# Graph-network layer in fp32: edge blocks turned in 32 by 32 squares on VectorE, and the last 24 blocks dealt singly by a clock of estimates

## The chip, the cores and the metric

The kernel runs on one core of a Trainium2 chip. The metric is the device time of one execution in microseconds (us). Before the change the median of three runs is 1333.0 us (1331.73 to 1334.65).

The core has several engines that run side by side and meet at semaphores: TensorE (PE in the profile; its weight loads are PEld), VectorE (DVE), ScalarE (ACT), GpSimd (POOL) and SyncE (SP, which here only issues transfers). Each engine takes its instructions in the order in which they were written into its own program. An instruction that waits holds up all that stand behind it on that engine.

## The reference

There are 8192 nodes with 256 channels, and 131072 edges sorted by their target node, each with 64 attributes. Cut to what matters:

```python
ea = edge_attr @ w_e + b_e
msg = relu(x[src] + ea)                       # gather of source rows
agg = segment_sum(msg, dst, num_segments=N)   # sum by target
t = x + agg
h_local = bn1(relu(t @ w1 + b1) @ w2 + b2 + x)
h_attn  = bn2(attention(x, groups of 32 nodes, 4 heads) + x)
out = h_local + h_attn
out = bn3(out + relu(out @ m_w1 + m_b1) @ m_w2 + m_b2)
return layernorm(x + out)
```

All of it is computed in float32.

## The kernel before

**Edges.** The 131072 edges are cut into 128 blocks of 1024 (`NB`, `BE`). A block's edges lie on 128 partitions in 4 groups `h` with 2 columns `j` each. For each block the kernel does this:

- `gather` (L134): 8 indirect transfers issued by GpSimd, each fetching 128 source rows of 1 KB into the tile `xs`. There are 4 such tiles in rotation, so the gather of block b+4 can't begin before block b has been added up. From block 20 (`NX`) on the rows come from `xb`, a copy of x with the edge bias already added, which the kernel makes in the first blocks (`copy_load`, `copy_store`, L547 to L553).
- `load_edges` (L149): the attributes of two blocks in one transfer of 512 KB from SP, in pieces of 512 bytes.
- `edge_transpose` (L167, L169): the matrix product needs attributes on partitions and edges along the row. TensorE turns the 4 groups of a block against the identity into a PSUM tile `tp`, and ScalarE copies them out to `eaT`.
- `edge_products` (L459; below block 20 also L467 for the bias): `eaT` times the edge weights, into two PSUM tiles `pe` of two banks each.
- `edge_messages` (L481, L485): VectorE adds `pe` and `xs` into `msg`, ScalarE applies the relu. Two additions a block; for the very last block four smaller ones.
- `edge_hot` (L490), `edge_sums` (L504, L510): TensorE multiplies a one-hot matrix of the targets with `msg`, which sums the edges of up to 32 neighbouring targets in each group (`pw`). ScalarE copies it to `ws`.
- `edge_place` (L522, L532): a second one-hot product moves the sums to their place among 160 node columns (`l2`), and VectorE adds them to `xT`, the transposed node features.

**Nodes.** The 8192 nodes are cut into 16 chunks of 512. For each chunk there are three generators: `attention_front` (L276 to L297), `attention_back` (L308 to L375) and `dense` (L391 to L444: the two local layers, the two layers of the MLP, the layer norm and the store). `dense` of a chunk can start once the last block that touches it has been placed. The last two chunks are cut into pieces: (14, tiles 0 to 2), (14, 2 to 4), (15, 0 to 2), (15, 2 to 3) and (15, 3 to 4).

**Order.** The program order of TensorE is the order in which this code calls (`manual_schedule`), that of VectorE and ScalarE is by hand only below block 26 (`NV`) and later left to a scheduler. The loop (L640 to L683) takes blocks in pairs, and the last 8 (`NS`) singly: products, additions, sums of the blocks before, products and additions of the second block, then node work, the turning of blocks b+2 and b+3, the placing, more node work. How much node work stands between is a budget in estimated microseconds (`Work.run`, 5.1 us a block, 4.2 below block 20), handed round the generators in turn.

**PSUM.** Eight banks: 2 for `at` (node work), 4 for `pe`, 1 shared by `tp` and `pw` (tag `sm`), 1 for `l2`.

Of the kernel before, what the change touches and what calls it, by code (L numbers as in the profile page):

```python
# [9 lines left out]
FP = mybir.dt.float32  # L10
# [8 lines left out]
P = 128  # L19
N, C, E, ED, H, NPG = 8192, 256, 131072, 64, 4, 32  # L20
DH = C // H
KC = C // P
BE = 1024
NB = E // BE
# [3 lines left out]
TB = NH * TJ  # L28
NPB = N // NB
# [10 lines left out]
NS = 8  # L40
# [11 lines left out]
def gnn_kernel(ctx: ExitStack, tc: tile.TileContext, x, src, dst, edge_attr, w, out):  # L52
# [7 lines left out]
    for b in range(ND):  # L60
        (nc.sync, nc.scalar)[b].dma_start(
            srcd[:, b * NH : (b + 1) * NH, :], src[b * BE : (b + 1) * BE].rearrange("(g p j) -> p g j", p=P, j=TJ)
        )
# [56 lines left out]
    def bank():  # L120
        return pps.tile([P, CH], FP, name="at", tag="at", bufs=2)
# [22 lines left out]
    def load_edges(b):  # L144

        if b % 2:
            return
        ea = epool.tile([P, 2, NH, TJ * ED], FP, name="ea", tag="ea", bufs=2)
        nc.sync.dma_start(  # L149
            ea.rearrange("p s h d -> p (s h) d"),  # L150
            edge_attr[b * BE : (b + 2) * BE, :].rearrange("(g p j) d -> p g (j d)", p=P, j=TJ),
        )
        for s in range(2):
            ea_of[b + s] = ea[:, s]
# [4 lines left out]
    load_edges(2)  # L159
# [3 lines left out]
    def edge_transpose(b):  # L163
        ea = ea_of.pop(b)
        tp = pps.tile([P, NH, P], FP, name="tp", tag="sm", bufs=1)
        for h in range(NH):
            nc.tensor.transpose(tp[:, h, :], ea[:, h, :], ident)  # L167
        eaT = epool.tile([P, NH, P], FP, name="eaT", tag="eaT", bufs=2)
        nc.scalar.copy(eaT, tp)  # L169
        eaT_of[b] = eaT  # L170

    with tc.tile_pool(name="setup", bufs=1) as sp:
# [17 lines left out]
        edge_transpose(0)  # L190
        edge_transpose(1)
        srcf = npool.tile([P, NH, P, TJ], FP, name="srcf", tag="zT")
        nc.vector.tensor_copy(srcf.rearrange("s h p j -> s (h p j)"), srci_r)
        for h in range(NH):
            ps = bank()[:, : TJ * NB].rearrange("p (j s) -> p j s", j=TJ)
            for j in range(TJ):
                nc.tensor.transpose(ps[:, j, :], srcf[:, h, :, j], ident)
# [33 lines left out]
        dstf = npool.tile([P, NH, P, TJ], FP, name="dstf", tag="oT")  # L231
        nc.vector.tensor_copy(dstf.rearrange("s h p j -> s (h p j)"), dsti_r)

        dst3 = dstf.rearrange("s h p j -> s h (p j)")
# [5 lines left out]
        for h in range(NH):  # L240
            ps = bank()[:, : TJ * NB].rearrange("p (j s) -> p j s", j=TJ)
            for j in range(TJ):
                nc.tensor.transpose(ps[:, j, :], dstf[:, h, :, j], ident)
# [205 lines left out]
    pe_of, msg_of, oh_of = {}, {}, {}  # L449

    def edge_products(b):

        eaT = eaT_of.pop(b)
# [361 lines left out]
```

## Time and profile before

| | |
|---|---|
| median of 3 runs | 1333.0 us |
| the profiled execution's own time | 1332.57 us |
| its span, first to last instruction | 1330.7 us |
| first gather starts, last gather's issue ends | 3.31 us, 1299.76 us |
| last row of the layer norm written (L441) | 1327.06 us |
| PE busy | 1234.3 us (93%) |
| DVE, ACT busy | 712.2 us (54%), 658.7 us (49%) |
| GpSimd busy in its 1024 gathers | 982.8 us of the three gather groups |
| mean TensorE clock granted | 0.986 of full speed |

Busy times add up over the whole span, and engines overlap. A busy share says little on what sets the end: an engine with a share of 74% can be the one that never stops, if the rest of its time is the gap between two of its own instructions that nothing else causes. The view of waits tells this: idle time put down to "issue" is time in which the engine waited for nothing that the profile shows.

### The profile page before, as it was taken

To read this page: it belongs to the slowest core of one execution; us is meant where nothing else is said; L and a number is where in the kernel's file an instruction comes from. 1 tells how busy PE (TensorE), PEld (TensorE's weight loads), DVE (VectorE), ACT (ScalarE), POOL (GpSimd) and SP (SyncE) were. 2 spreads that over 40 slices of the span, in tenths; PEclk is the share of its full clock that TensorE was granted. 3 is DMA by queue.
4 is the path that set the end of the run, shared out by engine and by line. 5 is a ranking of instruction groups with operands and counts; after the bars stand their busy time and mean duration, and the time that the engine had idled before them with its cause. 6 is when DMAs were issued, how large, how long until landed. Compare 5 with 4: busy or idle time off the path is not lost.

```text
span 1330.7 us, 21178 instructions
## 1 busy us (share of the span) xinstructions
PE 1234.3 (93%) x8307; PEld 783.6 (59%) x8307; DVE 712.2 (54%) x1202; ACT 658.7 (49%) x959; POOL 983.9 (74%) x1032
## 2 busy tenths in 40 slices
PE   4998979999999999899899999999898998989997
PEld 3766756655555556556556565555555565655665
DVE  4566554555537464644637464564636446454654
ACT  2535344465546455455546555463545445544443
POOL 7777777777777777777777777777777777777770
PEclk9998989999999999999999999999999999999999
DMA  8788655454545454454545454454445445444540
GB/s 279 251 277 272 198 149 151 135 159 130 168 137 153 135 166 126 132 170 125 165 137 150 138 169 136 121 169 138 151 138 151 135 138 150 136 136 139 159 116 30
DMA packets 140613, 206.77 MB, mean 155 GB/s; under 512 B 19646, under 2 KB 103900, under 8 KB 139740
## 3 DMA queue, kind: packets, MB, share of 16 engines
q0 software_dynamic: 49152, 134.28, 35.0%
q1 hardware_dynamic: 89468, 69.76, 16.8%
q10 hardware_dynamic: 1888, 1.32, 0.3%
q8 instruction: 67, 1.10, 0.3%
q14 instruction: 38, 0.31, 0.1%
HBM read 188.51 MB, written 16.78 MB: 154 GB/s over the span
## 4 chain that ended last, share of the span: by engine, by line
PE 56%; POOL 17%; issue 9%; DVE 8%; ACT 6%; DMA 4%; DVEq 0%; ACTq 0%; POOLq 0%
POOL xs L134 17%; PE at L391 16%; PE pe L459 11%; PE at L294 6%; PE pw L504 5%; PE l L522 3%; PE at L372 3%; DVE msg L481 3%; PE at L308 3%; PE tp L167 3%; PE pe L467 3%; DMA xs<-xb,srci 2%; PE at L360 2%; ACT pr L335 2%; DVE bd L352 1%
## 5 line engine op out<-in xcount | busy, mean ns | idle before, releaser
L134 POOL DMA_INDIRECT xs<-xb,srci x864 | 824.9, 955 | 263.8 <-issue 249.8
L485 ACT ACTIVATE msg<-msg 128x1024 f32<-128x1024 f32 (+1 forms) x258 | 270.9, 1051 | 329.5 <-DVE msg L481 320.7
L481 DVE TENSOR_TENSOR msg<-pe,xs 128x1024 f32<-128x1024 f32 (+1 forms) x258 | 304.7, 1211 | 174.5 <-PE pe L459 72.3
L459 PE MATMUL pe<-we,eaT 64*128 64x256 f32 x2048 | 262.3, 391 | 12.0 <-DVE msg L481 11.1
L459 PEld LDWEIGHTS pe<-we,eaT 64*128 64x128 f32 x2048 | 187.3, 187 | 99.7 <-issue 43.5
L134 POOL DMA_INDIRECT xs<-in_x_dram,srci x144 | 142.1, 987 | 45.3 <-issue 41.1
L391 PE MATMUL at<-hA,mw 128*128 128x512 f32 (+2 forms) x304 | 123.6, 533 | 3.4 <-ACT xT L284 2.0
L504 PE MATMUL pw<-msg,oh 128*32 128x256 f32 x2048 | 124.6, 382 | 0.0
L169 ACT COPY eaT<-tp 128x512 f32<-128x512 f32 x128 | 74.3, 581 | 100.0 <-PE tp L167 99.4
L294 PE MATMUL at<-xT,inT 128*128 128x512 f32 x256 | 122.7, 605 | 1.1 <-ACT xT L284 1.1
L391 PE MATMUL at<-m,mw 128*128 128x512 f32 (+2 forms) x304 | 117.4, 530 | 1.4 <-ACT m L407 1.4
L532 DVE TENSOR_TENSOR xT<-l,xT 128x352 f32<-128x352 f32 (+4 forms) x98 | 43.2, 463 | 96.0 <-PE l L522 96.0
L167 PEld LDWEIGHTS tp<-ident,ea 128*128 128x128 f32 x512 | 63.8, 144 | 49.9 <-issue 39.3
L504 PEld LDWEIGHTS pw<-msg,oh 128*32 128x32 f32 x2048 | 59.6, 109 | 54.6 <-issue 21.9
L167 PE MATMUL tp<-ident,ea 128*128 128x128 f32 x512 | 80.0, 280 | 11.8 <-DMA ea<-in_edge_attr_dram 6.1
L522 PEld LDWEIGHTS l<-oh,ws 128*128 128x128 f32 x512 | 74.1, 191 | 14.9 <-issue 13.5
L522 PE MATMUL l<-oh,ws 128*128 128x160 f32 x512 | 81.8, 301 | 0.5 <-ACT ws L510 0.5
L391 PEld LDWEIGHTS at<-m,mw 128*128 128x128 f32 x304 | 53.8, 190 | 48.0 <-issue 43.8
L391 PEld LDWEIGHTS at<-hA,mw 128*128 128x128 f32 x304 | 52.6, 190 | 49.1 <-issue 39.2
L294 PEld LDWEIGHTS at<-xT,inT 128*128 128x128 f32 x256 | 46.1, 192 | 50.2 <-issue 47.2
L391 PE MATMUL at<-xT,w 128*128 128x512 f32 (+2 forms) x152 | 64.8, 558 | 10.1 <-DVE y L431 4.7
L391 PE MATMUL at<-h,w 128*128 128x512 f32 (+2 forms) x152 | 65.5, 554 | 9.1 <-ACT h L398 6.4
(109 smaller groups left out, 1286.9 us busy)
## 6 DMA issues: line engine op xcount, KB each, us to landing
ea<-in_edge_attr_dram SPq DMA_DIRECT2D x64, 512.0 KB
xs<-xb,srci POOLq DMA_INDIRECT x864
xn<-in_x_dram SPq DMA_DIRECT2D x16, 512.0 KB
out_dram<-y SPq DMA_DIRECT2D x14, 512.0 KB
xp<-in_x_dram SPq DMA_DIRECT2D x10, 512.0 KB
xb<-xp SPq DMA_DIRECT2D x10, 512.0 KB
xp<-in_x_dram SPq DMA_DIRECT2D x3, 1024.0 KB
xb<-xp SPq DMA_DIRECT2D x3, 1024.0 KB
```

Of the source, the lines that this page charges most:

```text
L134: nc.gpsimd.indirect_dma_start(out=xs[:, h, j, :], out_offset=None, in_=x if b < NX else xb[:, :], in_offset=bass.IndirectOffsetOnAxis(ap= ...
L167: nc.tensor.transpose(tp[:, h, :], ea[:, h, :], ident)
L169: nc.scalar.copy(eaT, tp)
L294: nc.tensor.matmul(ps, inT[:, k, o * P : (o + 1) * P], xT[:, k, :], start=(k == 0), stop=(k == KC - 1))
L308: nc.tensor.matmul(ps[:, (t - t0) * C : (t - t0 + 1) * C], xT[:, k, t * P : (t + 1) * P], inT[:, k, 2 * C :], start=(k == 0), stop=(k == K ...
L391: nc.tensor.matmul(ps, wt[:, k, o * P : (o + 1) * P], act[:, k, :], start=(k == 0), stop=(k == nk - 1))
L459: nc.tensor.matmul(pe[:, i, u, :], eaT[rows, h + u, :], we[rows, :], start=(b >= NX or u == 0), stop=(b >= NX), skip_group_check=True,)
L481: nc.vector.tensor_add(msg[:, hs].rearrange("p u i c -> p i u c"), pe[:, :, u : u + n, :], xs[:, hs].rearrange("p u i c -> p i u c"),)
L485: nc.scalar.activation(msg[:, hs], msg[:, hs], AF.Relu)
L504: nc.tensor.matmul(pw[h * WN : (h + 1) * WN, i, :], oh[:, h * TJ + j, :], msg[:, h, j, :], start=(j == 0), stop=(j == TJ - 1), skip_group_ ...
L522: nc.tensor.matmul(l2[:, k, i * NPB : i * NPB + WB], ws[:, i, k * P : (k + 1) * P], oh2[:, i, :], start=(i == 0 and k == 0), stop=(i == la ...
L532: nc.vector.tensor_add(xT, l2[:, :, a - n : z - n], xT)
```

## The change

Four things change.

1. **Turning.** `edge_transpose` becomes one VectorE instruction per block, which turns each 32 by 32 square within its own 32 partitions; TensorE's 512 turnings, ScalarE's 128 copies and the PSUM tile `tp` go. That gives the wanted transpose only if the squares already stand on the right partitions: edge h*256 + j*128 + r*4 + m of a block stands in row r of two groups of 32 partitions, one for each half of the 64 attributes, and m and h count along the row. So `load_edges` now loads each block alone in 4 transfers of 32 partitions. Both halves are loaded by a transfer of the full rows, the second one shifted by 32 columns, so each attribute is fetched twice, in pieces of 1 KB. The index arrays (`srcd`, `srcf`, `dstf`) follow the new numbering; `srcd` is loaded in 8 transfers of single 4-byte elements where 2 transfers of 8-byte ones stood.
2. **PSUM.** The banks: 3 for `at` (2 before), 4 for `pe`, and 1 shared by `pw` and `l2`.
3. **The order up to block 103.** Turning of block b+2 now follows the products of block b at once (`next_edges`), and the placing stands at one place in each pair. The condition that a chunk's front waits for the placing of the chunk three before is dropped.
4. **The order from block 104 (`TAIL`) on.** Blocks go singly. A clock `t` of estimates is kept: `came` is when a block's rows are taken to have arrived, and each step of a block (products, additions, sums, placing) has an estimated due time. Whichever is due is written next; in between, `Work.step` writes one piece of node work. The additions of a block are put behind the newest copy of `ws` (ScalarE) and the newest addition to `xT` (VectorE) by `issue_after`.

```diff
-        return pps.tile([P, CH], FP, name="at", tag="at", bufs=2)
+        return pps.tile([P, CH], FP, name="at", tag="at", bufs=3)
...
+        ea = ea_of[b] = epool.tile([P, QR + NH * EQ * ED], FP, name="ea", tag="ea", bufs=2)
+        for j in range(TJ):
+            for i in range(ED // QR):
+                p0, c0 = j * ED + i * QR, (1 - i) * QR
+                nc.sync.dma_start(
+                    ea[p0 : p0 + QR, c0 : c0 + NH * EQ * ED].rearrange("r (g d) -> r g d", g=NH),
+                    edge_attr[b * BE : (b + 1) * BE, :].rearrange("(g j r m) d -> j r g (m d)", j=TJ, r=QR, m=EQ)[j],
+                )
...
-        tp = pps.tile([P, NH, P], FP, name="tp", tag="sm", bufs=1)
-        for h in range(NH):
-            nc.tensor.transpose(tp[:, h, :], ea[:, h, :], ident)
-        eaT = epool.tile([P, NH, P], FP, name="eaT", tag="eaT", bufs=2)
-        nc.scalar.copy(eaT, tp)
-        eaT_of[b] = eaT
+        eaT = eaT_of[b] = epool.tile([P, NH * EQ, QR], FP, name="eaT", tag="eaT", bufs=2)
+        nc.vector.transpose(eaT, ea[:, QR:].rearrange("p (g d) -> p g d", d=ED)[:, :, :QR])
...
+    def next_edges(b):
+        if b < NB:
+            edge_transpose(b)
+        if b + 2 < NB:
+            load_edges(b + 2)
...
-        l2 = pps.tile([P, KC, C], FP, name="l2", tag="l2", bufs=1)
+        l2 = pps.tile([P, KC, C], FP, name="l2", tag="pw", bufs=1)
...
+        came = [11.5 + 10.06 * (i + 1) for i in range(NB)]
+        t, p, m, s, l = came[b - 2] + 20, b, b, b - 2, b - 2
+        added = dict((i, came[i] + 2.0) for i in range(b))
...
+        while l < NB:
+            times = [1e9] * 4
+            if l < s:
+                times[0] = summed_at[l] + 1.5
+            elif s < m:
+                times[1] = max(added[s] + 1.2, bank_free)
+            if p < NB and m == p:
+                times[2] = added[p - 1]
+            if m < p:
+                times[3] = came[m]
+            if t >= times[0]:
+                edge_place(*sums)
...
+            elif t >= times[1]:
+                sums = edge_sums([s])
...
+            elif t >= times[2]:
...
+                edge_products(p)
+                next_edges(p + 2)
+                edge_hot(p)
...
+            elif t >= times[3]:
+                with ExitStack() as behind:
+                    for i in newest.values():
+                        behind.enter_context(tc.issue_after(i))
+                    edge_messages(m)
...
+            else:
+                t = work.step(t, min(times))
```

## The prediction

> **What bounds the kernel now.** I read the groups first. The row of the gathers carries the answer:
>
> ```profile
> L134 POOL DMA_INDIRECT xs<-xb,srci x864 | 824.9, 955 | 263.8 <-issue 249.8
> L459 PE MATMUL pe<-we,eaT 64*128 64x256 f32 x2048 | 262.3, 391 | 12.0 <-DVE msg L481 11.1
> L167 PE MATMUL tp<-ident,ea 128*128 128x128 f32 x512 | 80.0, 280 | 11.8 <-DMA ea<-in_edge_attr_dram 6.1
> L169 ACT COPY eaT<-tp 128x512 f32<-128x512 f32 x128 | 74.3, 581 | 100.0 <-PE tp L167 99.4
> ```
>
> Almost all the idle time before a gather is "issue". The view of GpSimd's waits says the same, and shows the one place where gathers waited for a free buffer:
>
> ```profile
> POOL xs L134 <- issue: 295.5, 970, 0.3
> POOL xs L134 <- DVE oh L513: 3.8, 6, 1.7
> POOL xs L134 <- DMA srcd<-in_src_dram: 1.7, 1, 1.7
> ```
>
> Then GpSimd's timeline, at the first gather, at block 18 and at the last:
>
> ```profile
> 3.31 1.10 POOL L134 DMA_INDIRECT xs<-in_x_dram,srcd  x1 [1.70 <-DMA srcd<-in_src_dram]
> ...
> 191.03 0.97 POOL L134 DMA_INDIRECT xs<-in_x_dram,srci  x1 [1.70 <-DVE oh L513]
> ...
> 1298.82 0.94 POOL L134 DMA_INDIRECT xs<-xb,srci  x1 [0.30 <-issue]
> ```
>
> From start to start a gather takes 1.25 us in the undisturbed stretches. 1024 of them from 3.31 us on would end at 1283; they end at 1299.76, so 16 us are lost to disturbances in all. This stream never stops, so before 1299.76 no other engine sets the time, PE with its 93% included: what PE saves there only makes the lag behind the gathers smaller. The end is the gather stream plus what follows it. Of the 30.9 us that follow (1330.7 - 1299.76), 3.64 are the last store and the close of the program (last row 1327.06, span 1330.7). The other 27.3 are work, and the timeline of the end shows how it stands:
>
> ```profile
> 1301.82 2.00 PE L459 MATMUL pe<-we,eaT 64*128 64x256 f32 x16
> 1303.75 1.07 PE L504 MATMUL pw<-msg,oh 128*32 128x256 f32 x16
> 1305.87 0.81 PE L522 MATMUL l<-oh,ws 128*128 128x160 f32 x4 [0.46 <-ACT ws L510]
> 1311.29 1.07 PE L504 MATMUL pw<-msg,oh 128*32 128x256 f32 x16
> 1314.46 0.71 PE L522 MATMUL l<-oh,ws 128*128 128x160 f32 x4
> 1315.20 0.39 DVE L532 TENSOR_TENSOR xT<-l,xT 128x224 f32<-128x224 f32 x1 [0.19 <-PE l L522]
> 1319.44 2.61 PE L391 MATMUL at<-hA,mw 128*128 128x128 f32 x16
> 1326.65 0.41 DVE L441 TENSOR_SCALAR y<-y,mv,rstd 128x256 f32<-128x256 f32 x1
> ```
>
> The rows of block 127 have landed at 1301.25 (last packet of the gathers' queue), but its products come only at 1301.82, its messages are complete at about 1306.3, its sums wait until 1311.29 behind node work written ahead of them, and it is placed at 1315.6. That is 14 us from landing to placed.
>
> **What the Trainium skill says.** "SBUF — State Buffer", section "Who interferes with whom", says that a VectorE instruction with one SBUF input outside the 2-port modes does not contend with GpSimd, while one with two SBUF inputs does contend with a GpSimd instruction that reads SBUF. The trace agrees: a fit of all 1024 gather spacings against what VectorE ran meanwhile gives 0.46 us lost per us of the additions at L552 (two SBUF inputs; 5.6 us in all) and 0.014 for the 64 square-turns at L352. "Perfetto Trace Analysis", section "GPSIMD Engine Instruction", says to time GpSimd by start-to-start spacing, as I did. "VectorE: DVE Perf Modes", section "The three transpose paths", says that VectorE turns 32 by 32 squares only, which is why the layout changes too; the time comes from L352, 701 ns at 512 elements a partition. "DMA: Bandwidth & Descriptors", section "Specifications", puts the least size for full rate at 512 bytes. The trace doesn't show a sharp edge there: packets of 512 bytes on SP's queue took 28.5 ns, of 1024 bytes 50.4.
>
> **The change part by part.**
>
> *Turning.* PE loses 512 x 0.28 = 80 us busy (4 of them take 0.66 us, so some 84), ScalarE 74 us, VectorE gains 128 x 0.70 = 90 us (712 becomes 802, 60% of the span). None of this is on the gather stream, which covers it. What reaches the stream: 90 us of new VectorE time at 0.014 is 1.3 us at most, zero at least; I take 0.7. In the first 60 blocks PE was the late engine: at block 18 the additions came 24 us after the rows, and the gathers of blocks 18 and 22 waited 1.70 and 0.85 us where 0.30 is usual. Those two waits, 1.95 us together, should go, since PE saves 0.66 us per block, 9 us by block 14. Against it, VectorE must turn block b+2 between the products and the additions of b, so the second additions come 0.7 us later; the sums (1.86 us) stand on PE meanwhile, so about 0.4 us a pair comes back. Bounds: 0 to -2.
>
> *Loads.* Each block takes 512 packets as before, twice as long: 512 x (50.4 - 28.5) ns / 16 engines = 0.7 us of 10 in DMA share, from 0.50 to 0.57 in the middle, from 0.85 to 0.92 in the first 60 us. SP issues 8 transfers a pair instead of 1, at about 0.4 us each; SP waits most of the time, so hidden. If not, edges come late, and the stream notices only when a lag of three blocks is used up.
>
> *Start.* This lies on the stream. The first gather waited for one `srcd` transfer, issued from 0.75 to 1.20 us. Now it waits for two on each of two queues, so for a second issue of about 0.45 us. The elements for block 0 are 1024, as many as both old transfers had together (9 ns each). I take +0.4, bounds +0.2 and +1.2. Behind these stand the loads that the third block's indices need (`srci_r`, landed about 12.6, `dsti_r` 15.5). Eight attribute transfers, each waiting for an earlier transfer (SP's waits show the custom: L178 stood 1.7 us for `we`), now stand ahead of them on SP, which puts them about 2 us later; a cast with a strided read and three casts follow. Before, the last was done at 20.5 and needed at 23.97. So 1.5 us of slack remain: 0 taken, up to +2 if it is used up.
>
> *Order to block 103 and PSUM.* No instruction is added. A third `at` bank and a single `pw`/`l2` bank move waits on PE, which the stream covers; 0.
>
> Gather end: 1299.76 + 0.4 - 1.95 + 0.7 = 1298.9. The 13 copy additions collide with gathers by chance, which may be 3 us either way.
>
> *The tail.* In the written order of the new program, TensorE's last items are: products 127, sums 126, 4 matmuls, placing 126, first layers of piece (15, 2 to 3), sums 127, 4 matmuls, placing 127, the rest. I time it on the old landing, 1301.25. Three of the four small additions of block 127 need only earlier rows, so after landing remain one addition (0.62), a relu (0.63) and about 0.3 of signals: 1302.8. But the mlp matmuls written before the sums need two operations that stand behind that addition on VectorE (0.35 each): sums at 1303.5 to 1304.5, `ws` copy (0.37) to 1305, placing behind 4 matmuls (1.16) from 1305.7 to 1306.4, addition to `xT` (0.39) done at 1306.9, against 1315.6. After that the old program needs 3.8 us to the mlp of the last piece (1315.65 to 1319.44) and 7.6 more to the last row. The new one writes more of piece (15, 2 to 3) in between: 0.6 first layer, 0.6 mlp, 0.6 first layer, 1.1 second mlp layer, 0.6 second layer, 1.1 mlp, 0.6 second layer, 0.4 turning, plus 0.5 of latency, 6.1 instead of 3.8. So 1306.9 + 6.1 + 7.6 = 1320.6: the last row 20.8 us after the last gather issue instead of 27.3, a gain of 6.5. What was late, the placing of block 127, is no longer; next late is PE itself with two pieces to finish. Bounds of the gain: 1 (the order stalls, below) and 9 (the last piece's matmuls run as tightly as before).
>
> *Sum.* 1298.9 + 20.8 + 3.64 = a span of 1323.3 us. The profiled execution took 1332.57 with a span of 1330.7, so 1.9 lie around it; the median of the runs, 1333.0, is 2.3 over the span. Predicted: 1325.6. What a measurement of this kernel can tell from no change is about 0.2%, 2.7 us: 1330.3 to 1335.7.
>
> **Rivals.**
>
> *The order doesn't fit the arrivals.* The clock takes block 127 to come at 1299.2, block 103 at 1057.7; the old trace has 1301.25 and 1060.2. If that holds, TensorE reaches products and sums two us early and stands, with ready node work behind it; VectorE stands too, at the second addition of each block. PE has 10 us a block and, by the written list, up to 9.8 us of work, so lost time piles up over some blocks. For it: PE can't overtake. Against: a constant offset is lost once, and pieces of node work fall due in between. Then about 1 to 5 us of the gain remain: 1327 to 1332, likeliest 1330.
>
> *A faster stream as well.* If the copy additions collide less and the start costs nothing, 1298.9 becomes 1295 to 1297, and with a tail gain of 7 the time is 1319 to 1323. For it: 5.6 us of collisions are there to lose. Against: their number does not change.
>
> *Slower: the new turns hold up GpSimd.* They are wider than those at L352 (128 partitions, 32 there) and read with a stride. If they cost the stream as the additions at L552 do, it is 90 x 0.46 = 41 us: 1366. It decides for "slower" from (7.4 + 2.7) / 90 = 0.11 us per us on. Against: 64 turns in the trace began and ended over gathers almost without a trace. Late edges in the first 20 blocks, with DMA near its full share, would end on the same side, but would need over 10 us of waits on the stream.
>
> **How the numbers follow.** Forecast (1323 to 1328.5): 0.60. Faster stream: 0.14. Misfit order: 0.16, half of it below 1330.3. Slower: 0.10. So faster 0.60 + 0.14 + 0.08 = 0.82, same 0.08, slower 0.10. The range takes the forecast, most of the faster stream and of the misfit: 1319.5 to 1332.
>
> **What would show it.** Right: gathers 1.25 us apart, no gap over 0.3 at blocks 18 and 22, last issue ending at 1297 to 1301; a start at about 3.7; 128 turns of about 0.7 us; block 127 placed 6 to 8 us after its last gather's issue ended (15.8 before); last row about 21 us after it. Wrong: gathers stretched while VectorE turns; a wait for `srci` near 24 us; waits of TensorE for additions of VectorE in each block after 104; idle PE in the last 20 us.

## The result, and the profile after

The changed kernel takes 1329.73 us (median of 22 runs, 1325.28 to 1332.04). The kernel before, run beside it, takes 1331.67 us (22 runs, 1330.07 to 1335.54). The ratio is 0.9984 [0.9977, 0.9991]: 1.9 us faster, under a third of the 7.4 us forecast, and less than the 0.2% that the prediction called a difference. The profiled execution took 1331.09 us with a span of 1329.3.

The mechanisms of the change are in the profile. These are the rows of the page that answer to those of before:

```profile
PE 1195.2 (90%) x7795; PEld 741.0 (56%) x7795; DVE 784.9 (59%) x1339; ACT 587.7 (44%) x840; POOL 983.9 (74%) x1032
...
L138 POOL DMA_INDIRECT xs<-xb,srci x864 | 823.7, 953 | 263.2 <-issue 250.1
...
L169 DVE STREAM_TRANSPOSE eaT<-ea 128x512 f32<-128x512 f32 x128 | 90.1, 704 | 99.6 <-PE pe L459 70.9
```

128 turns cost VectorE 90.1 us, at 704 ns each. The gathers on GpSimd are as long as before (953 ns, 955 before), and a fit of the durations of all 1024 gathers against what VectorE ran meanwhile gives -0.004 us lost per us of the turns (0.012 in `k1_start`, below). So the turns don't hold them up. But GpSimd's timeline shows where the forecast was lost. Shown are the first gather, the last of block 1 with the first of block 2, the first of block 4, that of block 18, and the last of all:

```profile
4.25 1.10 POOL L138 DMA_INDIRECT xs<-in_x_dram,srcd  x1 [2.65 <-issue]
...
23.16 1.80 POOL L138 DMA_INDIRECT xs<-in_x_dram,srcd  x1 [0.30 <-issue]
25.87 1.47 POOL L138 DMA_INDIRECT xs<-in_x_dram,srci  x1 [0.92 <-DVE srci L198]
...
49.30 0.94 POOL L138 DMA_INDIRECT xs<-in_x_dram,srci  x1 [3.22 <-DVE msg L487]
...
197.06 0.96 POOL L138 DMA_INDIRECT xs<-in_x_dram,srci  x1 [1.68 <-DVE oh L519]
...
1302.79 0.95 POOL L138 DMA_INDIRECT xs<-xb,srci  x1 [0.30 <-issue]
```

Before, the gathers of blocks 2 and 4 followed at the usual 0.30 us. Now block 2 waits for its indices and block 4 for a buffer that the additions of block 0 release. Besides, the last gather of block 1 and the first of block 2 take 1.80 and 1.47 us, where 0.95 is usual. Under the first of them VectorE casts `srci_r`, which it reads with a stride since the change:

```profile
23.06 1.07 DVE L193 CAST srcf<-srci_r 128x1024 f32<-128x1024 int32 x1 [1.24 <-DMA srci_r<-in_src_dram]
```

Under the second it casts `dsti_r` in the same way. Before, the two casts took 0.69 and 0.93 us, and the longest gathers beside them 1.21 and 1.02. The stream ends at 1303.74 us, 3.97 later than before (1299.76), where 0.9 earlier was predicted. Taking 1.251 us, the median spacing, as undisturbed, these are the us lost beyond it:

| stretch of the stream | before | after | difference |
|---|---|---|---|
| start of the first gather | 3.31 | 4.25 | +0.94 |
| gathers of blocks 0 to 3, up to the first of block 4 | 0.63 | 5.02 | +4.39 |
| blocks 4 to 19 | 7.26 | 7.63 | +0.37 |
| blocks 20 to 127 | 7.85 | 6.12 | -1.73 |
| sum | | | +3.97 |

So the whole loss lies in the first 50 us. Of the 4.39 us, 0.6 are the wait of block 2, 2.9 that of block 4, and 0.9 the longer gathers. SyncE's timeline shows what the two waits come from. First the kernel before:

```profile
1.25 1.12 SPq L149 DMA_DIRECT2D ea<-in_edge_attr_dram  x2
3.21 0.61 SPq L177 DMA_DIRECT2D srci_r<-in_src_dram  x1
5.53 0.34 SPq L178 DMA_DIRECT2D dsti_r<-in_dst_dram  x1
```

Then the changed kernel, and under it the first row of its waits of SyncE's queue between 0 and 40 us (us in total, times, longest):

```profile
2.67 12.54 SPq L154 DMA_DIRECT2D ea<-in_edge_attr_dram  x8
15.26 0.43 SPq L176 DMA_DIRECT2D srci_r<-in_src_dram  x1
15.73 0.43 SPq L177 DMA_DIRECT2D dsti_r<-in_dst_dram  x1
```

```profile
SPq L154 <- DMA in_r<-in_L_gnn_in_w_dram: 5.1, 1, 5.1
```

Eight attribute loads took 12.5 us to be issued, and the last of them stood 5.1 us for `in_r`, a weight load on ScalarE's queue that nothing in the code links with it. `srci_r` is issued 12 us later than before. The first node rows `xn` follow on the same queue at 30.64 us (20.29 before), and TensorE stands for them ahead of its first products:

```profile
37.80 1.94 PE L283 MATMUL at<-ident,xn 128*128 128x128 f32 x8 [2.75 <-DMA xn<-in_x_dram]
```

The first products run at 42.3 us instead of 32.2, and the additions of block 0 end at 49.0 instead of 37.2, so the 6.7 us that its buffer had to spare are gone. Of these 11.8 us, 0.9 came as the first eight products took 2.04 us instead of 1.14, at half clock: the granted clock was 0.50 from 33.9 to 44.1 us in this execution, 1.00 in the kernel before. Another 0.9 came as VectorE now turns block 2 before it adds up block 0.

The length of the end, in contrast, came nearly as predicted. From the timeline of the end, after products 127 (which now stand ahead of the last rows):

```profile
1296.18 2.00 PE L459 MATMUL pe<-we,eaT 64*128 64x256 f32 x16
...
1308.84 1.94 PE L510 MATMUL pw<-msg,oh 128*32 128x256 f32 x16
...
1312.58 1.27 PE L528 MATMUL l<-oh,ws 128*128 128x160 f32 x4
...
1313.89 0.39 DVE L538 TENSOR_TENSOR xT<-l,xT 128x224 f32<-128x224 f32 x1 [4.76 <-PE l L528]
...
1325.21 0.41 DVE L441 TENSOR_SCALAR y<-y,mv,rstd 128x256 f32<-128x256 f32 x1
```

The last row is written 21.9 us after the last gather's issue ended (27.3 before, 20.8 predicted). A gain of 5.4 us at the end stands against a loss of 4.0 in the stream. The clock was at half here too, for 6.8 us from 1307.1 on: from the start of the sums to the placed block it took 5.4 us, and 3.1 in `k1_start`, where it was at 1.00.

### The profile page after: what moved, and what is told of

Its sections match the earlier page's. It is cut to its first block, busy times and chain, and to the rows that moved or that the text cites. A ratio compares the mean times of both kernels' runs of the same rounds, so it can differ in the third digit from the quotient of the medians.

```text
span 1329.3 us, 21099 instructions
## 1 busy us (share of the span) xinstructions
PE 1195.2 (90%) x7795; PEld 741.0 (56%) x7795; DVE 784.9 (59%) x1339; ACT 587.7 (44%) x840; POOL 983.9 (74%) x1032
## 3 DMA queue, kind: packets, MB, share of 16 engines
q10 hardware_dynamic: 2448, 1.32, 0.4%
## 4 chain that ended last, share of the span: by engine, by line
PE 38%; POOL 28%; issue 14%; DVE 9%; DMA 8%; ACT 2%; DVEq 0%; ACTq 0%; SPq 0%; POOLq 0%
POOL xs L138 28%; PE at L391 11%; PE pe L459 8%; DMA xs<-xb,srci 5%; PE at L294 5%; PE pw L510 4%; DVE msg L487 3%; PE l L528 3%; PE at L372 2%; PE pe L467 2%; PE at L308 1%; DMA xp<-in_x_dram 1%; PE at L360 1%; PE pe L325 1%; DMA in_r<-in_L_gnn_in_w_dram 1%
## 5 line engine op out<-in xcount | busy, mean ns | idle before, releaser
L459 PE MATMUL pe<-we,eaT 64*128 64x256 f32 x2048 | 271.0, 398 | 29.8 <-DVE msg L487 26.4
L459 PEld LDWEIGHTS pe<-we,eaT 64*128 64x128 f32 x2048 | 192.1, 191 | 118.5 <-issue 74.6
L169 DVE STREAM_TRANSPOSE eaT<-ea 128x512 f32<-128x512 f32 x128 | 90.1, 704 | 99.6 <-PE pe L459 70.9
L510 PE MATMUL pw<-msg,oh 128*32 128x256 f32 x2048 | 130.4, 389 | 6.6 <-DVE oh L496 5.0
L528 PEld LDWEIGHTS l<-oh,ws 128*128 128x128 f32 x512 | 78.0, 196 | 28.4 <-issue 21.9
L528 PE MATMUL l<-oh,ws 128*128 128x160 f32 x512 | 87.9, 312 | 2.0 <-ACT ws L516 2.0
L538 DVE TENSOR_TENSOR xT<-l,xT 128x96 f32<-128x96 f32 (+4 forms) x107 | 46.1, 452 | 54.2 <-PE l L528 53.9
L391 PE MATMUL at<-xT,w 128*128 128x512 f32 (+2 forms) x152 | 70.9, 606 | 6.9 <-DVE xT L538 6.9
L407 ACT ACTIVATE m<-at,vec 128x512 f32<-128x512 f32 (+2 forms) x76 | 46.8, 616 | 57.2 <-PE at L391 56.7
L297 ACT ACTIVATE qk<-at,vec 128x512 f32<-128x512 f32 x64 | 43.6, 684 | 62.6 <-PE at L294 62.4
```

The lines of the kernel that those rows point to most:

```text
L169: nc.vector.transpose(eaT, ea[:, QR:].rearrange("p (g d) -> p g d", d=ED)[:, :, :QR])
L297: nc.scalar.activation(qk[:, o, :], ps, AF.Identity, bias=v_("in_b", o))
L391: nc.tensor.matmul(ps, wt[:, k, o * P : (o + 1) * P], act[:, k, :], start=(k == 0), stop=(k == nk - 1))
L407: nc.scalar.activation(m1[:, o, :], layer(mw1, KC, o, hA), AF.Relu, bias=v_("m_b1", o))
L459: nc.tensor.matmul(pe[:, i, u, :], eaT[rows, h + u], we[rows, :], start=(b >= NX or u == 0), stop=(b >= NX), skip_group_check=True,)
L510: nc.tensor.matmul(pw[h * WN : (h + 1) * WN, i, :], oh[:, h * TJ + j, :], msg[:, h, j, :], start=(j == 0), stop=(j == TJ - 1), skip_group_ ...
```

## The experiments

**Theory:** SyncE's first loads cost the stream its 4 us, and the end's gain is real. **Rivals:** the order by the clock eats its own gain; the wider turns and finer loads lengthen the stream over its whole length; the order of the end needs nothing of the other parts.

One thing about the chips has to be known. The 18 kernels ran on five chips. On four of them (all runs but `k1_start`, `k2_start_old_tail` and `k3_new_tail_only`) even the kernel before takes 2015 to 2107 us. TensorE's work takes longer there (busy for 1423 us in `f1_as_is`, at a mean granted clock of 0.834; 1195 us in the changed kernel, at 0.967), and it stands for 200 to 290 us for "issue", that is, for nothing that the profile can name. An example from `h1_light`, where the turns of `in_r` and `out_r` stand 2 to 5 us for "issue":

```profile
30.57 0.69 PE L207 MATMUL at<-ident,in_r 128*128 128x128 f32 x2 [2.62 <-issue]
33.42 0.69 PE L207 MATMUL at<-ident,in_r 128*128 128x128 f32 x2 [2.17 <-issue]
38.35 0.31 PE L212 MATMUL at<-ident,vec_r 30*128 30x30 f32 x1 [4.24 <-issue]
43.25 0.69 PE L207 MATMUL at<-ident,out_r 128*128 128x128 f32 x2 [4.59 <-issue]
```

On those chips the gathers wait some 560 to 760 us, most of it for buffers that the additions release, and TensorE bounds the kernel. They are used only for what SyncE, the transfers and the first indices do, and for a comparison of ratios near the end. Times at the scale of 1330 us come from the fifth chip; which chip the result itself came from isn't known.

### The first loads in another order

```diff
     gather(0)
-    load_edges(0)
     gather(1)
-    load_edges(1)
...
         nc.sync.dma_start(srci_r, src.rearrange("(s e) -> s e", s=NB))
         nc.sync.dma_start(dsti_r, dst.rearrange("(s e) -> s e", s=NB))
+        load_edges(0)
+        load_edges(1)
+        for c in range(2):
+            xn_of[c] = npool.tile([P, TN, C], FP, name="xn", tag="xn", bufs=4)
+            nc.sync.dma_start(xn_of[c], x[ds(c * CH, CH), :].rearrange("(t p) c -> p t c", p=P))
```

`attention_front` takes `xn` from `xn_of` for chunks 0 and 1. Nothing else differs from the changed kernel.

> The changed kernel with SyncE's first loads in the other order (srci_r and dsti_r right behind srcd, then the edge loads of blocks 0 and 1, the xn loads of chunks 0 and 1, the biases, the edge loads of blocks 2 and 3). Where the kernel before takes 1330 to 1335 us: no wait over 0.3 us before blocks 2 and 4, first products at 29 to 34 us, last gather's issue ends 1299 to 1301 instead of 1303.7, last row 21 to 23 us after it, 1324.5 to 1327.5 us. Rival (the tail dealt by the clock eats its own gain): 1328.5 us or more.

Measured: 1326.2 us (1323.82 to 1326.96), against 1332.0 for the kernel before on the same chip; ratio 0.9944 [0.9926, 0.9962]. SyncE's timeline, and GpSimd's at the first gather, at blocks 2, 4 and 18 and at the last:

```profile
2.68 0.45 SPq L174 DMA_DIRECT2D srci_r<-in_src_dram  x1
3.75 0.35 SPq L175 DMA_DIRECT2D dsti_r<-in_dst_dram  x1
4.42 12.16 SPq L154 DMA_DIRECT2D ea<-in_edge_attr_dram  x8
17.97 0.95 SPq L180 DMA_DIRECT2D xn<-in_x_dram  x2
```

```profile
4.32 1.10 POOL L138 DMA_INDIRECT xs<-in_x_dram,srcd  x1 [2.72 <-issue]
...
26.11 0.95 POOL L138 DMA_INDIRECT xs<-in_x_dram,srci  x1 [0.30 <-issue]
...
46.12 0.95 POOL L138 DMA_INDIRECT xs<-in_x_dram,srci  x1 [0.30 <-DVE eaT L167]
...
192.86 0.96 POOL L138 DMA_INDIRECT xs<-in_x_dram,srci  x1 [0.41 <-DVE oh L525]
...
1298.55 0.95 POOL L138 DMA_INDIRECT xs<-xb,srci  x1 [0.30 <-issue]
```

The edge loads still take 12 us to issue, but the indices stand ahead of them. The waits at blocks 2 and 4 are gone, that of block 18 has shrunk from 1.68 to 0.41, the stream ends at 1299.50 (4.2 sooner), and the last row is again 21.9 us behind it (1321.40). First products ran at 37.4 us, later than the 29 to 34 expected, because the biases now stand behind the `xn` loads (their turning came at 30.8 us); it is early enough. The median is 3.5 us under that of the changed kernel, and the intervals of the two ratios don't overlap. So the theory holds, and the rival that the order of the end eats its gain falls. This version beats both kernels.

There are three limits. The run moves indices, node rows and biases together and doesn't tell what each is worth. In its profile the clock was at 1.00 through the first 60 us, so a part of the difference to the changed kernel's profile (about 0.9 us of block 4's wait) may be the clock's. And blocks 0 to 3 still lose 1.8 us (0.63 before), all of it in stretched gathers: those beside the two casts take 1.68 and 1.38 us here too.

The same kernel ran on two of the other chips, beside the changed kernel as it stands on the first of them, and a simpler form, with only the index loads moved, on another:

> The changed kernel as it stands, beside the three others. Both theories: 1328 to 1331.5 us, last gather's issue ending 1303 to 1304.5, last row 21 to 23 us after it.

> The changed kernel with SyncE's first loads in another order: srci_r and dsti_r right behind srcd, then the edge loads of blocks 0 and 1, then the xn loads of chunks 0 and 1, then the biases, then the edge loads of blocks 2 and 3. Theory (the late index loads and late xn loads cost the stream of gathers its 4 us): srci casts done before 22 us, no wait over 0.3 us before blocks 2 and 4, first products at 29 to 34 us instead of 42, last gather's issue ends 1299 to 1301 instead of 1303.7, last row still 21 to 23 us after it: 1324.5 to 1327.5 us, 3 to 4 under the changed kernel as it stands. Rival (the tail dealt by the clock eats its own gain, or the lower clock does): the waits at blocks 2 and 4 may go, but the time stays within 1 us of the changed kernel as it stands.

> The changed kernel in full, with SyncE's first loads in the other order, once more. Where the gathers bound the kernel (the kernel before at 1330 to 1335 us): no wait over 0.3 us before blocks 2 and 4, first products at 29 to 34 us instead of 42, last gather's issue ends 1299 to 1301 instead of 1303.7, last row 21 to 23 us after it: 1324.5 to 1327.5 us, ratio to the kernel before 0.994 to 0.998. Rival (the tail dealt by the clock eats its own gain): 1328.5 us or more. Where TensorE bounds it (the kernel before over 1900 us): a ratio of 0.985 to 0.995, and neither theory is told apart by it.

> The changed kernel with one thing moved: the two loads of all edge indices (srci_r, dsti_r) stand ahead of the first two blocks' attribute loads on SP. Theory A (the start-up costs the stream: index loads held back 12 us on SP behind attribute loads that wait for earlier transfers): the waits before blocks 2 and 4 (0.92 and 3.22 us) shrink to 0.3, the last gather's issue ends at 1299 to 1301 instead of 1303.7, the time falls by 3 to 4 us, to about 1326. Theory B (the stream lost its time to VectorE's turns and the doubled attribute bytes in the first 20 blocks): the waits only move to later blocks, the last issue stays at 1302.5 or later, the time within 1.5 us of the changed kernel's.

`f1_as_is` 1992.66 us (ratio 0.9889 [0.9851, 0.9927]), `f2_start` 2000.27 (0.9907 [0.9871, 0.9943]), `h4_start` 2035.52 (0.9652 [0.9576, 0.9728]), `e1_index_first` 2020.07 (0.9639 [0.9598, 0.968]). The times expected were missed by far, since TensorE was the bound; `h4_start` also missed the ratio of 0.985 to 0.995 that was expected for such a chip. The indices can be compared all the same: `srci_r` was issued at 13.28 us in `f1_as_is` and at 2.67 to 2.72 in the other three, and the last cast of `srci` ended at 26.9 us against 14.9 to 16.4. In `e1_index_first` the `xn` loads stayed behind the edge loads and the biases and left at 42.3 us, no sooner than in `f1_as_is` (40.2); moving the indices alone did not bring them forward.

### Why eight loads take 12 us

Here the same semaphore numbers come back in the records of SyncE's and ScalarE's transfers: eight of them, dealt in rotation over both queues, each transfer waiting until the earlier user of its semaphore has landed. To test this, `in_r` is moved to SyncE behind `dsti_r`, so that it takes its semaphore after the edge loads:

```diff
-        nc.scalar.dma_start(in_r, w["in_w"].rearrange("(o p) c -> p o c", p=P))
+        nc.sync.dma_start(in_r, w["in_w"].rearrange("(o p) c -> p o c", p=P))
```

To take TensorE out, it ran in a light form, beside the changed kernel and the other order of loads in the same form. Only the first of the accumulated products of the projections, the dense layers and the sums is computed, so what it returns isn't the layer's output:

```diff
-            for k in range(nk):
+            for k in range(1):
...
-            for j in range(TJ):
+            for j in range(1):
                 for h in range(NH):
                     nc.tensor.matmul(pw[...], oh[...], msg[...])
```

> The changed kernel with TensorE's load cut: of the attention's projections, the four dense layers and the sums of edges only the first of the accumulated products is computed, so that the output isn't the reference's. The order on every engine is kept, and the gathers should bound it on any chip. Theory (the stream's 4 us come from the first loads): start at 4.2 to 4.4 us, the cast of srci_r at 21 to 24 us and a wait of 0.3 to 1.5 us before block 2, a wait of 1 to 5 us before block 4, last gather's issue ends 1301 to 1304.5. Rival (the stream is lengthened over its whole length by the turning on VectorE or the finer edge loads, or by TensorE's work in the middle): no such waits at the start, or a mean spacing over 1.258 us from block 20 on.

> As h1_light, with SyncE's first loads in the other order (srci_r and dsti_r right behind srcd, then the edge loads of blocks 0 and 1, the xn loads of chunks 0 and 1, the biases, the edge loads of blocks 2 and 3). Theory: cast of srci_r at 6.5 to 8 us, no wait before block 2, a wait before block 4 of 0 to 0.5 us, last gather's issue ends 1298.5 to 1300.5, 2.5 to 4.5 before h1_light's. Rival: within 1 us of h1_light.

> As h1_light, but in_r is loaded on SyncE's queue behind dsti_r, not on ScalarE's ahead of everything; the edge loads still stand in front of srci_r. Theory (the eighth edge load waits 5 us because the semaphore that it takes in rotation still belongs to in_r): that wait goes, srci_r is issued at 8.5 to 10.5 us instead of 13 to 15.5, the cast of srci_r starts at 15 to 19 us, no wait before block 2; the products come no sooner, so that 1 to 5 us of wait before block 4 stay. Rival (eight edge loads simply take that long to issue): srci_r is still issued after 12.5 us.

They took 1890.13, 1890.19 and 1891.91 us. TensorE was busy for 1060.6 us (`h1_light`) instead of 1434.5 (`f2_start`, on another such chip), but the gathers still waited some 560 us (last issue at 1852 to 1855 us, waits before block 4 of 15 to 17 us), so the ends of the stream that were expected tell nothing. SyncE's first 15 us do. `h1_light`:

```profile
2.69 11.65 SPq L154 DMA_DIRECT2D ea<-in_edge_attr_dram  x8
14.38 0.43 SPq L176 DMA_DIRECT2D srci_r<-in_src_dram  x1
```

and `h3_light_in_r`:

```profile
2.74 6.85 SPq L154 DMA_DIRECT2D ea<-in_edge_attr_dram  x8
11.79 0.35 SPq L176 DMA_DIRECT2D srci_r<-in_src_dram  x1
```

With `in_r` away, the eight loads take 6.9 us instead of 11.7. `srci_r` leaves 2.6 us sooner, at 11.79 and not at the 8.5 to 10.5 expected, because it now meets `out_r` in the rotation (a wait of 2.2 us); its cast starts at 18.5 us (21.9 in `h1_light`), and the first gather of block 2 follows at 0.30 us, at 25.60. (It did in `h1_light` too, at 25.74, behind gathers that the casts had stretched to 1.80 and 1.34 us.) So 4.8 of the 12 us are this one load, and the rival that eight loads simply take that long falls. In `h2_light_start` the cast of `srci_r` started at 6.8 us.

### The order of the end

The changed kernel with the first loads mended, but with the end as before: pairs to block 120, then single blocks by the budget, no clock, additions not held back.

```diff
-TAIL = 104
+TAIL = 120
...
-        came = [11.5 + 10.06 * (i + 1) for i in range(NB)]
...
-                t = work.step(t, min(times))
+        while b < NB:
+            ...
+            edge_products(b)
+            next_edges(b + 2)
+            edge_messages(b)
+            if waiting:
+                sums = edge_sums(waiting)
+            ...
+            work.run(0.5 * per)
+            b += 1
```

> As k1_start, with blocks from 104 on in the order of the kernel before (pairs to 120, then singly by the budget, no clock, additions not held behind placing). Where the kernel before takes 1330 to 1335 us: stream as in k1_start, last row 26 to 28 us after the last gather's issue, 1329.5 to 1332 us, 4.5 to 6 over k1_start. Rival (the order of the end is worth nothing): within 1 us of k1_start.

Measured: 1332.78 us (1329.23 to 1335.0), ratio 1.0001 [0.9989, 1.0013], and 6.6 us over `k1_start`. So the other three parts together, with mended loads, are worth nothing that shows (1.7 us either way), and by the medians the whole gain comes with the order of the end; time and difference lie just over the bounds expected. The profiled execution was one of the faster (1331.07 us): its stream ends at 1300.21, its last row is 24.7 us behind, less than expected; against `k1_start`'s profile that is 2.8 us at the end, 0.7 in the stream and 0.7 behind the last row. So in this execution the end was 2.6 us shorter than before the change (27.3) without the clock's order. How the other runs come to the median's 6.6 isn't seen in a profile.

> As f2_start, and blocks from 120 on in the order of the kernel before (in pairs to 120, then singly, by the budget, without the clock and without the additions held behind placing). Theory: stream as in f2_start, last row 26 to 28 us after the last gather's issue instead of 21 to 23: 1329.5 to 1332 us, 4.5 to 6 over f2_start. Rival (the tail's order is worth nothing here): within 1 us of f2_start.

> The changed kernel with the old order at the end: pairs up to block 119, the last 8 singly by budget, no clock, no issue_after; turning, loads and PSUM as changed. If the clock's order is what shortened the end, the last row comes 26 to 28 us after the last gather's issue (21.9 in the changed kernel) and the time rises by 4 to 6 us, to 1334 to 1336. If a lighter TensorE (no turning) alone did it, the last row comes 22 to 23.5 us after and the time stays within 1.5 us.

Where TensorE is the bound these two took 2002.27 us (0.9954 [0.9908, 1.0]) and 2028.26 (0.9676 [0.9633, 0.9718]), within half a per cent of their neighbours with the new end.

### The order of the end alone

The kernel before, with TensorE turning the edges, its loads and its banks, and only the order from block 104 on from the change (and the condition on a chunk's front dropped):

```diff
-NS = 8
+TAIL = 104
...
+        came = [11.5 + 10.06 * (i + 1) for i in range(NB)]
...
                 edge_products(p)
-                next_edges(p + 2)
+                if p + 2 < NB:
+                    edge_transpose(p + 2)
                 edge_hot(p)
                 t += 2.1
```

(The last hunk is against the changed kernel.)

> The kernel before, with only the order from block 104 on taken from the change. Where the kernel before takes 1330 to 1335 us: last gather's issue ends 1299 to 1300.5 as in the kernel before, last row 21 to 23.5 us after it, 1325 to 1328 us. Rival (it is the turning on VectorE that lets TensorE follow at the end): last row 25 to 27 us after the last issue, 1329 to 1332 us.

Measured: 1358.53 us (1358.0 to 1360.2), ratio 1.0191 [1.0174, 1.0208]: 26.5 us slower than the kernel before. Neither theory had this. In the view of GpSimd's waits, and in its timeline at block 122, the gathers wait for buffers again, and the chain that ended last runs through TensorE:

```profile
POOL xs L134 <- DVE oh L513: 11.4, 13, 3.7
POOL xs L134 <- DVE msg L481: 7.3, 10, 4.4
```

```profile
1246.30 0.94 POOL L134 DMA_INDIRECT xs<-xb,srci  x1 [4.40 <-DVE msg L481]
```

```profile
PE 58%; POOL 13%; DVE 9%; issue 8%; ACT 6%; DMA 4%; DVEq 0%; ACTq 0%; POOLq 0%
```

In `k1_start` the same line begins with POOL 35%, PE 24%. From the first products of block 104 to those of block 122 TensorE needs 199.7 us, in `k1_start` 171.8. The lines are those of the products, `k1_start` first:

```profile
1075.78 0.49 PE L465 MATMUL pe<-we,eaT 64*128 64x256 f32 x2
...
1247.55 0.49 PE L465 MATMUL pe<-we,eaT 64*128 64x256 f32 x2
```

```profile
1079.10 0.49 PE L459 MATMUL pe<-we,eaT 64*128 64x256 f32 x2
...
1278.82 0.70 PE L459 MATMUL pe<-we,eaT 64*128 64x256 f32 x4
```

That is 11.1 us a block, where rows come every 10.06, against 9.5. Between these points the two programs hold the same matmuls in the same number, but for 72 turns, 4 more of the mlp and 8 fewer at L308, a projection of the attention. Of the 27.9 us more, 16.7 are busy time (the turns 11.8 of it) and 11.2 are gaps (19.9 against 8.6). In 5.0 us of its gaps sums wait for ScalarE's copy of turned edges: as before the change, turning and sums share a PSUM bank here. The lag of the additions behind the rows grows from 10 us at block 105 to 36 at block 119, until the gathers themselves wait, and the end follows 45 us behind the last gather instead of 27. The clock counts 2.1 us for a block's products and nothing for turning. It deals out node work for a TensorE that doesn't turn.

Whether the uncounted turns overfill TensorE, or the gaps would do it too, was to be told by counting the turns (2.8 instead of 2.1 us):

```diff
-                t += 2.1
+                t += 2.8
```

> k3_new_tail_only (the kernel before with the order of the end from the change, 1358.5 us), with one number of the clock changed: a block's products count 2.8 us instead of 2.1, so that TensorE's turning of a block, 0.66 us, is counted. Where the kernel before takes 1330 to 1335 us: theory (the order gives TensorE more per block than the 10 us it has, because it doesn't count the turning): the lag of the additions stays below 15 us after block 104, no gather waits there, last issue ends 1299 to 1301, last row 22 to 28 us after it, 1326 to 1333 us. Rival (other waits make TensorE late: the PSUM bank that turning and sums share, ScalarE's copies of the turned edges in its queue): the lag still grows past 20 us, 1340 us or more.

It ran on a chip where TensorE is the bound: 2101.39 us, ratio 1.0003 [0.9981, 1.0024]. So it stays open which of the parts that this kernel lacks (turning on VectorE, the loads, the banks) the order needs. Two more runs of the order alone were on such chips too:

> The kernel before with edges turned by TensorE as there and only the order of the end from the change (blocks from 104 on singly by the clock, additions behind placing, the front's condition dropped). Theory: stream as in the kernel before (last issue ends 1299 to 1300.5), last row 21 to 23.5 us after it: 1325 to 1328 us, 4 to 6 under the kernel before. Rival (the turning on VectorE is what lets TensorE follow at the end): last row 25 to 27 us after the last issue, 1329 to 1332 us.

> The kernel before (turning on TensorE, its loads and PSUM banks) with the clock's order from block 104 on. If the two parts are independent, the stream ends as before (1299.8), the last row comes about 22.5 us after it, and the time is 4 to 5 us under the kernel before: about 1327, faster than the whole change. If the clock's order needs a TensorE without turning, its 0.66 us per block and the shared bank make TensorE late at the end: last row 24 to 27 us after, time within 2.5 us of the kernel before.

2007.78 us (0.996 [0.9939, 0.9981]) and 2081.46 (0.9944 [0.992, 0.9969]). On these chips a pattern shows: kernels whose edges VectorE turns stand at 0.964 to 0.968 of the kernel before on three of them, and at 0.989 to 0.995 on the fourth; kernels whose edges TensorE turns at 0.994 to 1.000. There TensorE's time is what counts. Between kernels on one chip the turning, with its loads and banks, is worth about 3 to 3.6% on two of them and under 1% on the third.

### Two smaller questions

`srcd` in 4 transfers, both blocks in each, instead of 8, on top of `k1_start`:

```diff
-    for b in range(ND):
-        for m in range(EQ):
-            (nc.sync, nc.scalar)[m % 2].dma_start(
-                srcd[m * QR : (m + 1) * QR, b * NH : (b + 1) * NH, :],
+    for m in range(EQ):
+        (nc.sync, nc.scalar)[m % 2].dma_start(
+            srcd[m * QR : (m + 1) * QR, :, :],
```

> k1_start with srcd loaded by 4 transfers (both blocks in each) instead of 8. Where the kernel before takes 1330 to 1335 us: first gather starts at 3.2 to 3.9 us instead of 4.3, the stream ends 0.3 to 1 us sooner, last row 21 to 23 us after it: 1325 to 1326 us, below both the kernel before and the changed kernel. Rival (the first gather waits for the time of the small packets and not for the number of issues): start still at 4.1 us or later, within 0.5 us of k1_start.

The first gather started at 4.92 us, later than the 4.22 to 4.43 of the kernels with 8 transfers on those chips. So the theory falls: with fewer issues the start didn't come sooner. Whether the larger transfers or `srci_r`, which now leaves at 1.73 us, hold it up isn't told apart. The time, 2032.05 us (0.9655 [0.9607, 0.9704]), says nothing at this scale.

The additions not held behind the newest `ws` and `xT`:

```diff
-                with ExitStack() as behind:
-                    for i in newest.values():
-                        behind.enter_context(tc.issue_after(i))
-                    edge_messages(m)
+                edge_messages(m)
```

> k1_start without the additions held behind the newest copy of ws and the newest addition to xT, so that the scheduler puts them where it will on VectorE. Where the kernel before takes 1330 to 1335 us: theory (TensorE's order by the clock is what brings the end forward, holding the additions back adds little): within 1.5 us of k1_start, 1325 to 1328 us. Rival (additions that wait for rows hold up VectorE's work for sums and placing): last row 24 us or more after the last issue, 1329 us or more.

> The changed kernel without issue_after: from block 104 on the scheduler may put a block's additions ahead of the placing of the block before. If that order matters, VectorE stands at an addition whose rows have not landed while a placed sum waits behind it: the last row comes 2 to 4 us later after the last gather, time up by 2 to 4 us. If it does not, within 1 us of the changed kernel.

2026.79 us (0.9639 [0.958, 0.9698]) and 2021.78 (0.9654 [0.9601, 0.9707]), both where TensorE was the bound: no different from the kernels beside them. What holding the additions back is worth where the gathers bound the kernel wasn't measured.

## Why the prediction was wrong

The direction was right, the size was not: 1.9 us instead of 7.4.

**Start: the step that failed.** It said that eight attribute loads would put `srci_r` "about 2 us later", left 1.5 us of slack and booked 0. Measured: 12 us later. The step counted issues and knew of the waits, as it named one of 1.7 us, but didn't ask for what each of eight new transfers would wait. The row that would have told it stands in the view of the kernel before, in SyncE's waits:

```profile
SPq L188 <- DMA in_r<-in_L_gnn_in_w_dram: 7.5, 1, 7.5
```

There, a small load of biases waited 7.5 us for `in_r`, with nothing urgent behind it. Adding eight transfers ahead moved that wait in front of the indices. The second omission is the one that cost more: the step followed SyncE's queue as far as the indices and not to the `xn` loads behind them, on which the first products and so the buffer of block 0 hang. The start of the first gather was +0.94 to +1.0 instead of +0.4, within its bounds. All told the term is +5.3 us (0.94 + 4.39) where 0.4 was taken. Of it, 0.9 is in gathers beside the two casts: "a cast with a strided read" was named as a link of the chain, not as something that stretches a gather. Some 0.9 more goes with the half clock in the profiled execution. The prediction did name "a wait for `srci` near 24 us" as a sign of being wrong; it came at 25.

**Turning and loads.** 704 ns a turn as read, and ScalarE's busy time fell by 71 us (74 worked out). TensorE's fell by 39 us and not by 80: the turns went, but products, sums and placings took 20.6 us longer, at a mean clock of 0.967 instead of 0.986. VectorE's rose to 785 us, not 802. The DMA share between 200 and 800 us rose from 0.51 to 0.66, not to 0.57, as the packets of 1024 bytes on SyncE's queue took 62.9 ns on average and not 50.4; the stream from block 20 on doesn't show it. The two waits at blocks 18 and 22 should vanish: that of block 22 did, that of block 18 stayed at 1.68 as long as the start was late, and shrank to 0.41 once it was mended. The rival that turns hold up GpSimd (1366 us) falls: from block 20 on the stream loses 1.7 us less than before. What "Who interferes with whom" of "SBUF — State Buffer" in the Trainium skill says of VectorE with one SBUF input agrees with this for the turns. The two casts have one SBUF input too, and gathers were stretched beside them; the page excepts 2-port modes, and whether the casts ran in one isn't seen in a trace here.

**Order to block 103.** Booked at 0. `k2_start_old_tail` at 1.0001 agrees for the sum of everything but the end; alone this part wasn't measured.

**The tail.** Near in its sum, 21.9 instead of 20.8 us, and off in two terms that cancel, which is luck. Block 127 was placed 10.5 us after the last issue, not 7.1. In `k1_start`, whose rows landed at 1300.9 (1301.25 in the prediction), all four additions of block 127 ran after the landing, from 1301.95 on, behind the addition of block 126 to `xT`. The fourth ran at 1305.22 instead of about 1302, as VectorE did layer norm between them, and the sums at 1306.93. In the changed kernel the fourth ran 0.6 us after its rows had landed, but these landed 2.3 us after the last issue (1.4 in `k1_start`), and the half clock then cost 2.3 us. That both ends take 21.9 us is therefore chance. From the placing to the last row took 11.3 us in both, instead of 13.7. The rival that the order doesn't fit the arrivals isn't borne out: rows of block 127 landed 6.9 us after the clock's time in the changed kernel and 1.8 in `k1_start`, and the gain at the end was 5.4 us. Of its signs, TensorE did stand idle for 3.3 us between 1300 and 1308, but it didn't wait for additions in each block after 104 (3 waits in the products, 3.0 us in all).

**The sum, with the one term mended.** `k1_start` has the stream's end at 1299.50 (1298.9 predicted), the end at 21.9 (20.8) and the time at 1326.2 (1325.6). The median is off by 0.6 us, the profile's span by 1.8 (1325.1 instead of 1323.3). That the stream's end is so near is luck in part: start and blocks 0 to 3 cost 2.2 us where 0.4 was taken, and the blocks from 4 on gave back 2.4 where 1.25 was taken. Of the 4.1 us that the forecast missed, 3.5 lie between this kernel and the changed one.

**What it lacked besides.** It treated turning and the end's order as separate terms, one worth 1.3 us in the stream and the other 6.5 at the end. `k3_new_tail_only` and `k2_start_old_tail` show that they aren't: the order without the rest of the change loses 26.5 us, the rest without the order gains none by the median.

## What to carry to other kernels

When a change puts more transfers on a queue, follow that queue to the first thing that each engine needs from it, and look up what each transfer already waits for there; a long wait with nothing urgent behind it is a price that falls due when something urgent is moved behind it. A part of a change that is worth nothing alone may still be what another part lives on: the order of the end gained 6.6 us with the rest (and mended loads) and lost 26.5 without it. An order dealt by estimates may fit only the work that its estimates count; that this is the reason for the loss wasn't shown.

## What was unexpected of the hardware

- In these programs the transfers of SyncE and ScalarE share eight semaphores in rotation, so a 768 KB weight load on one queue held up a 128 KB load on the other by 5.1 us.
- The kernel before takes 1330 us on one chip and 2000 to 2100 on four others, where TensorE is busy longer and stands at ready work. Cutting its work didn't free it: the light kernels, with 1060.6 us of busy TensorE, still took 1890 us, at a mean granted clock of 0.75.
- The mean granted clock fell from 0.986 to 0.967 with the change, though TensorE was busy 39 us less. In these two profiles it falls in stretches at 0.50 of 3.4 to 10.2 us each: 10 in the profile of the kernel before, 17 in that of the changed one, two of them where it hurts, over the first products and over the last placing. In the second the sums took 1.94 us and the placing 1.27, against 1.07 and 0.71 in `k1_start`. What sets a stretch off wasn't tested.
- In each of the 15 kernels with the new numbering the strided casts of `srci_r` and `dsti_r` took 1.05 to 1.13 us, and the longest gathers beside them 1.22 to 1.84 and 1.34 to 1.69 us, where 0.95 is usual. In the 5 with the old numbering the casts took 0.69 to 0.93 us and these gathers 1.11 to 1.29 and 1.01 to 1.32. That the stride is the cause is likely, but no run changed it alone.
